# Routing of a mixture-of-experts block: one product for channels and logits, and choices marked by GpSimd

## The chip, the cores and the metric

The kernel runs on one core of one Trainium2 chip. The metric is the time of one execution on the device, in microseconds (us). The profile was taken by the hardware profiler in one further execution; its engines are PE (TensorE, with PEld for its weight loads), DVE (VectorE), ACT (ScalarE), POOL (GpSimd) and SP (SyncE, which issues DMAs).

## The reference

The input is a batch of 32 images of 128 channels and 56 x 56 pixels, so 100,352 tokens of 128 channels, all in fp32. The first layer is a depthwise convolution, a layer norm over channels, and a mixture of eight experts of which each token takes two, within a capacity. The second layer is an attention within each token and a second mixture of 64 experts. The change touches only how the first mixture chooses its experts:

```python
x = (x - mu) / jnp.sqrt(var + 1e-06) * ln_gamma + ln_beta
xf = x.reshape(T, C)
logits = xf @ Wg + bg
topv, topi = jax.lax.top_k(logits, K)          # K = 2 of E = 8
wts = jax.nn.softmax(topv, axis=-1)
priority = wts[:, 0]
order = jnp.argsort(-priority)
...
cap = int(CAP_RATIO * T / E)
pos = ...   # place of each choice in its expert, in order of priority
keep = pos < cap
```

A token has a place in an expert only if it is among the first `cap` tokens of that expert by priority.

## The kernel before, in words

The kernel has stages that follow each other. The convolution writes its channels to `conv_d` in device memory. Routing reads them back and finds each token's logits and its two experts. A selection stage then finds, by a search of 24 steps, the priority from which each expert keeps its tokens. After it come the scattering of tokens to experts, the experts, and the second layer.

Routing works on groups of seven tiles of 128 tokens, 112 groups in all. The generator `route(g)` writes the work of one group in steps that are parted by `yield`; `in_turn` starts one new group in each round and advances every group under way by one step, the oldest first. The steps before the change are:

1. load the group's channels into `ct` (L358, SyncE's queue, four buffers);
2. for each tile, multiply it with `jm` (L364), the matrix that takes off the mean over channels, into PSUM tiles `pc` of four and three tiles; ScalarE squares them and sums (`sq` L372 for four tiles, `sqs` L367 for three, which VectorE sums at L368) into `ss`; and multiply each tile again, with the eight columns of `rw` for the logits (L377), into the PSUM tile `pl`;
3. the inverse root of the variance, in `inverse`: three steps on ScalarE (L143 to L145);
4. four steps on GpSimd (L147 to L150), which leave it in `rst`;
5. VectorE multiplies `pl` by `rst` (L381) and adds the bias `cb` (L382), which gives the logits `lgs`;
6. VectorE finds the largest values (L387) and their indices (L389), tile by tile, and ScalarE copies the first two of each into `pk` (L390, L391).

In all these products the tile of `ct` is the stationary operand, which is loaded, and `jm` or `rw` is streamed. Before the groups, a few products of the weights set up `rw` and `cb` (L345 to L351, through the PSUM tile `pa`).

The selection stage takes the values and indices from `pk`. It computes the share and the priority of every token (`ex`, `den`, `share`, `prio`, L405 to L413; the negative largest logit `negl` on GpSimd, L410), and then for each expert a row of keys, `key[:, e, :]`, which holds the priority where the expert is one of the token's two and zero elsewhere (L418, L419, L422), less a constant (L423, ScalarE). The search counts over these rows (L447, L452).

Within an engine, instructions run in the order in which the scheduler of the framework put them, which weighs the steps of different groups against each other; waits between engines are semaphores that it places. PSUM tiles and SBUF tiles of a pool are buffers in turn, and a new use waits for the last reader of the old one.

Of the kernel before, what the change touches and what calls it, by code (L numbers as in the profile page):

```python
# [8 lines left out]
F32 = mybir.dt.float32  # L9
I32 = mybir.dt.int32  # L10
U32 = mybir.dt.uint32
AF = mybir.ActivationFunctionType
ALU = mybir.AluOpType
AX = mybir.AxisListType
# [3 lines left out]
P = 128  # L18
GJ = 7
# [6 lines left out]
def conv_attn_hybrid_kernel(  # L26
# [24 lines left out]
    nc = tc.nc  # L51
    N, C, H, W = x.shape
    HW = H * W
    T = N * HW
    E = Wg.shape[1]
# [19 lines left out]
    TC = T // P  # L75
# [43 lines left out]
    def over(t, n):  # L119
        return t.unsqueeze(2).to_broadcast([t.shape[0], t.shape[1], n])  # L120

    def across(t, n):
        return t.unsqueeze(1).to_broadcast([t.shape[0], n, t.shape[1]])
# [12 lines left out]
    def by_tile(t):  # L136
        return t.rearrange("c (j p) -> c j p", p=P)
# [61 lines left out]
    with tc.tile_pool(name="cv_c", bufs=1) as cc, tc.tile_pool(  # L199
        name="cv", bufs=3  # L200
# [20 lines left out]
        for c in range(C):  # L221
# [15 lines left out]
            for kw in range(KS):  # L237
                for r in range(2):
                    rows = slice(r * HP, r * HP + H)
                    for b in range(2):  # L240
# [4 lines left out]
                            start=(kw == 0),  # L245
                            stop=(kw == KS - 1),
# [17 lines left out]
    RO = C + C + E  # L264
    CHUNKS = ((0, 4), (4, GJ))
# [5 lines left out]
    rst = ch.tile([P, TC], F32, name="rst")  # L271
    lgs = ch.tile([P, TC, E], F32, name="lgs")
# [37 lines left out]
    count = ch.tile([P, P // E], F32, name="count")  # L310
# [7 lines left out]
    rw = ch.tile([C, RO], F32, name="rw")  # L318
    cb = ch.tile([P, C + E], F32, name="cb")

    pairs = ExitStack()
    pk = pairs.enter_context(tc.tile_pool(name="pairs", bufs=1)).tile([P, TC, 4], F32, name="pk")
    with tc.tile_pool(name="rt_c", bufs=1) as cc, tc.tile_pool(
        name="rt", bufs=4
    ) as rt, tc.tile_pool(name="rt_p", bufs=2, space=PSUM) as rtp:
        tc.keep_in_program_order(
            nc.scalar.preload_act_table_set("natural_log_exp_and_others")
        )
        gam = cc.tile([C, 1], F32, name="gam")
        nc.sync.dma_start(gam, ln_gamma.unsqueeze(1))  # L330
        nc.sync.dma_start(bet, ln_beta.unsqueeze(1))
        wg = cc.tile([C, E], F32, name="wg")
        nc.sync.dma_start(wg, Wg)
        bgt = cc.tile([P, E], F32, name="bgt")
        nc.sync.dma_start(bgt, bg.partition_broadcast(P))

        jm = cc.tile([C, C], F32, name="jm")
        nc.vector.tensor_scalar(jm, ident, 1.0 / C, None, ALU.subtract)
        raw = cc.tile([C, RO], F32, name="raw")
        nc.vector.tensor_copy(raw[:, :C], ident)  # L340
        nc.vector.tensor_copy(raw[:, C : C + C], turn)
        nc.vector.tensor_copy(raw[:, C + C :], wg)

        ps = rtp.tile([P, RO], F32, name="pa", bufs=1)
        nc.tensor.matmul(ps, bet.to_broadcast([C, P]), raw, start=True, stop=True)  # L345
        nc.vector.tensor_copy(cb[:, :C], ps[:, :C])
        nc.vector.tensor_tensor(cb[:, C:], ps[:, C + C :], bgt, ALU.add)
        nc.vector.tensor_scalar(raw, raw, gam, None, ALU.mult)
        ps = rtp.tile([P, RO], F32, name="pa", bufs=1)
        nc.tensor.matmul(ps, jm, raw, start=True, stop=True)  # L350
        nc.vector.tensor_copy(rw, ps)  # L351

        def route(g):
            pr, gl = divmod(g, GPP)
            cols = slice(g * GJ, (g + 1) * GJ)
            ct = rt.tile([C, GT], F32, name="ct")
            for im, px, col, n in segments(gl):
                nc.sync.dma_start(ct[:, col : col + n], conv_d[2 * pr + im, :, px : px + n])  # L358
            yield
            ss = rt.tile([P, GJ], F32, name="ss")  # L360
            for i, (j0, j1) in enumerate(CHUNKS):
                ps = rtp.tile([P, 4, C], F32, name="pc", bufs=4)
                for j in range(j0, j1):
                    nc.tensor.matmul(ps[:, j - j0, :], by_tile(ct)[:, j, :], jm, start=True, stop=True)  # L364
                if i:
                    sq = rt.tile([P, GJ - 4, C], F32, name="sqs", bufs=2)
                    nc.scalar.activation(sq, ps[:, : j1 - j0, :], AF.Square)  # L367
                    nc.vector.tensor_reduce(ss[:, j0:j1], sq, AX.X, ALU.add)  # L368
                else:
                    for j in range(j0, j1):  # L370
                        sq = rt.tile([P, C], F32, name="sq", bufs=2)
                        nc.scalar.activation(  # L372
                            sq, ps[:, j - j0, :], AF.Square, accum_out=ss[:, j : j + 1]
                        )
            pl = rtp.tile([P, GJ, E], F32, name="pl")
            for j in range(GJ):
                nc.tensor.matmul(pl[:, j, :], by_tile(ct)[:, j, :], rw[:, C + C :], start=True, stop=True)  # L377
            yield
            yield from inverse(rt, ss, 0, "rst", 3, rst[:, cols])
            lg = lgs[:, cols, :]  # L380
            nc.vector.tensor_tensor(lg, pl, over(rst[:, cols], E), ALU.mult)  # L381
            nc.vector.tensor_tensor(lg, lg, across(cb[:, C:], GJ), ALU.add)  # L382
            yield
            m8 = rt.tile([P, GJ, 8], F32, name="m8")
            i8 = rt.tile([P, GJ, 8], U32, name="i8")
            for j in range(GJ):
                nc.vector.max(m8[:, j, :], lg[:, j, :])  # L387
            for j in range(GJ):
                nc.vector.max_index(i8[:, j, :], m8[:, j, :], lg[:, j, :])  # L389
            nc.scalar.copy(pk[:, cols, 0:2], m8[:, :, 0:2])  # L390
            nc.scalar.copy(pk[:, cols, 2:4], i8[:, :, 0:2])  # L391

        in_turn(route(g) for g in range(NG))

    with tc.tile_pool(name="sel", bufs=1) as se, tc.tile_pool(
        name="sel2", bufs=2
# [1 line left out]


        HALF = 2.0**23
        ea = [pk[:, :, 2], pk[:, :, 3]]
        ex = se.tile([P, TC], F32, name="ex")
        nc.vector.tensor_tensor(ex, pk[:, :, 1], pk[:, :, 0], ALU.subtract)  # L405
        nc.scalar.activation(ex, ex, AF.Exp)
# [4 lines left out]
        prio = se.tile([P, TC], F32, name="prio")  # L411
# [3 lines left out]
        nc.vector.memset(less, -HALF)  # L415
        key = se.tile([P, E, TC], F32, name="key")
        for e in range(E):
            nc.vector.tensor_scalar(key[:, e, :], ea[0], float(e), None, ALU.is_equal)  # L418
            nc.vector.scalar_tensor_tensor(  # L419
                key[:, e, :], ea[1], float(e), key[:, e, :], ALU.is_equal, ALU.add  # L420
            )
            nc.vector.tensor_tensor(key[:, e, :], key[:, e, :], prio, ALU.mult)  # L422
            nc.scalar.activation(key[:, e, :], key[:, e, :], AF.Identity, bias=less)  # L423

        def total(cnt):
# [13 lines left out]
        for b in range(1, 25):  # L439
            step = 2.0 ** (24 - b)  # L440
            off = s2.tile([P, E - EV], F32, name="off")
# [4 lines left out]
            for e in range(EV):  # L446
                nc.vector.tensor_scalar(  # L447
                    junk[0], key[:, e, :], cand[:, e : e + 1], None, ALU.is_ge, ALU.add,
                    accum_out=cnt[:, e : e + 1],
                )  # L450
            for e in range(EV, E):
                nc.scalar.activation(  # L452
                    junk[1], key[:, e, :], AF.Sign, bias=off[:, e - EV : e - EV + 1],
                    accum_out=cnt[:, e : e + 1],
# [21 lines left out]
        for e in range(E):  # L476
            k = key[:, e, :]
            eq = se.tile([P, TC], F32, name=f"eq{e}")
            if e < 5:
# [3 lines left out]
                    accum_out=ngt[:, e : e + 1],  # L483
# [47 lines left out]
        ps = sep.tile([P, JB, E], F32, name="gram", tag="tot")  # L531
# [11 lines left out]
        ps = sep.tile([P, E, E], F32, name="sizes", tag="tot")  # L543
# [1055 lines left out]
```

## Time and profile before

| | |
|---|---|
| time, median of 3 runs | 9506.17 us (9501.17 to 9524.23) |
| time of the profiled execution | 9507.39 us |
| its span, first to last instruction | 9505.7 us |
| PE busy, share of the span | 8565.6 us, 90% |
| PEld busy | 6983.3 us, 73% |
| DVE busy | 6481.0 us, 68% |
| ACT busy | 5277.1 us, 56% |
| POOL busy | 6777.5 us, 71% |
| convolution, from the timeline | 0 to 703 us |
| routing | 703 to 1073 us |
| keys of the selection | 1073 to 1108 us |
| rest of the selection and start of the scatter | 1108 to 1330 us |

The shares of the whole span mix stages with different limits. The edited code runs only from 703 to 1108 us, so the stretch to read is that one, and in it the engine that is never idle.

### The profile page before, as it was taken

The page shows a single profiled execution, that of the slowest core. Times are in us where ns is not written, and L with a number is a line of the kernel's source. Part 1 is how long each engine was busy: PE and PEld are TensorE (multiplying, and loading weights), DVE is VectorE, ACT ScalarE, POOL GpSimd, SP SyncE. Part 2 cuts the span into 40 slices and gives each one's busy share as a digit, 9 for nine tenths or more (in the row PEclk, how much of TensorE's full clock was granted, in tenths as well). Part 3 has the DMA queues.
Part 4 walks back from the last instruction along what each step waited for, and adds up shares of the span by engine and source line. Part 5 has one row for each costly group of instructions (what it writes and reads, how often), then busy time and mean ns, then how long its engine had stood idle before and what let it go on. Part 6 is the DMA issues. An engine that isn't in the chain of part 4 may idle for free. (4 is left out here: it accounts for less than half of the span.)

```text
span 9505.7 us, 165321 instructions
## 1 busy us (share of the span) xinstructions
PE 8565.6 (90%) x62216; PEld 6983.3 (73%) x62216; DVE 6481.0 (68%) x10957; ACT 5277.1 (56%) x13401; POOL 6777.5 (71%) x4884
## 2 busy tenths in 40 slices
PE   9999558775999999998999999999999999999878
PEld 3459546554766666666889899988989988989733
DVE  1117889885222222225999999999999999999623
ACT  1116644332333333334788888888888888888600
POOL 0002137777787777777999999999999999999500
PEclk9999779998999999999999999999999999999865
DMA  9994238775444444442000000000000000000199
GB/s 205 213 205 142 70 103 226 209 210 150 77 62 71 71 69 69 70 65 39 25 31 31 31 28 26 29 31 31 31 31 25 29 30 31 31 31 31 62 317 336
DMA packets 996146, 849.92 MB, mean 89 GB/s; under 512 B 525013, under 2 KB 880664, under 8 KB 975859
## 3 DMA queue, kind: packets, MB, share of 16 engines
q1 hardware_dynamic: 470162, 494.25, 18.6%
q0 software_dynamic: 177664, 188.81, 11.5%
q10 hardware_dynamic: 347520, 156.28, 6.1%
q8 instruction: 493, 8.08, 0.4%
q14 instruction: 307, 2.51, 0.1%
HBM read 486.34 MB, written 353.64 MB: 88 GB/s over the span
## 5 line engine op out<-in xcount | busy, mean ns | idle before, releaser
L161 POOL TENSOR_TENSOR s<-s,q 128x2048 f32<-128x2048 f32 x784 | 3601.9, 4605 | 137.8 <-DVE s L161 107.5
L161 ACT ACTIVATE s<-s 128x2048 f32<-128x2048 f32 x784 | 1500.8, 1914 | 685.9 <-POOL s L161 682.2
L161 POOL DMA_INDIRECT t_d<-ys,xe x992 | 1530.5, 1543 | 409.2 <-issue 229.0
L161 DVE TENSOR_TENSOR s<-kv,c 128x2048 f32<-128x2048 f32 x784 | 1786.5, 2279 | 8.0 <-POOL c L161 8.0
L161 DVE TENSOR_TENSOR ev<-s,kv 128x2048 f32<-128x2048 f32 x784 | 1784.0, 2276 | 2.4 <-ACT s L161 2.4
L161 PE MATMUL sm<-ident,ev 128*128 128x128 f32 x12544 | 1530.6, 276 | 45.4 <-DVE ev L161 45.4
L161 PE MATMUL sm<-ident,s 128*128 128x128 f32 x12544 | 1526.1, 275 | 8.5 <-ACT s L161 8.5
L161 PEld LDWEIGHTS sm<-ident,ev 128*128 128x128 f32 x12544 | 1436.3, 144 | 92.8 <-DVE ev L161 50.6
L161 PEld LDWEIGHTS sm<-ident,s 128*128 128x128 f32 x12544 | 1405.0, 143 | 20.8 <-ACT s L161 8.7
L888 ACT ACTIVATE hT<-ph,b1t 128x512 f32<-128x512 f32 (+1 forms) x992 | 679.3, 685 | 1236.5 <-PE ph L884 1220.8
L899 DVE TENSOR_TENSOR ys<-py,b2t 128x512 f32<-128x512 f32 (+1 forms) x248 | 171.4, 691 | 1545.9 <-PE py L894 1454.2
L894 PEld LDWEIGHTS py<-w,hT 128*128 128x128 f32 x7936 | 960.6, 192 | 202.1 <-issue 91.5
L894 PE MATMUL py<-w,hT 128*128 128x128 f32 x7936 | 984.6, 278 | 0.2
L884 PE MATMUL ph<-xeT,w 128*128 128x512 f32 (+1 forms) x1984 | 921.3, 597 | 69.5 <-DVE xeT L880 69.5
L697 POOL DMA_INDIRECT xb_d<-xs,rd x784 | 766.5, 978 | 240.2 <-issue 199.2
L241 PE MATMUL cps<-xin,br 56*64 56x448 f32 x7168 | 687.5, 541 | 13.6 <-DVE br L235 11.1
L884 PEld LDWEIGHTS ph<-xeT,w 128*128 128x128 f32 x1984 | 348.3, 190 | 392.0 <-issue 293.2
L241 PEld LDWEIGHTS cps<-xin,br 56*64 56x64 f32 x7168 | 334.0, 132 | 366.4 <-issue 331.2
L161 PE MATMUL pa<-rw,ct 128*128 128x256 f32 x1568 | 393.4, 393 | 127.6 <-DVE xs L161 127.5
L287 POOL MEMSET code<- 128x64 f32 x1 | 0.2, 151 | 697.4 <-DMA conv_d<-ot 697.4
L161 PEld LDWEIGHTS pa<-rw,ct 128*128 128x128 f32 x1568 | 283.7, 194 | 261.0 <-DVE xs L161 172.0
L161 PE MATMUL kv<-wq,zT 128*128 128x256 f32 x1568 | 417.2, 389 | 52.7 <-DVE ev L161 52.3
(330 smaller groups left out, 13264.5 us busy)
## 6 DMA issues: line engine op xcount, KB each, us to landing
ct<-conv_d SPq DMA_DIRECT2D x192, 448.0 KB
xin<-in_x_dram SPq DMA_DIRECT2D x256, 196.0 KB
conv_d<-ot ACTq DMA_DIRECT2D x512, 98.0 KB
t_d<-xs ACTq DMA_DIRECT2D x112, 448.0 KB
tr<-t_d SPq DMA_DIRECT2D x112, 448.0 KB
to<-t_d SPq DMA_DIRECT2D x32, 1568.0 KB
out_dram<-oo ACTq DMA_DIRECT2D x32, 1568.0 KB
xg<-in_x_dram SPq DMA_DIRECT2D x96, 448.0 KB
```

The source lines that it names most:

```text
L161: r = getattr(self.engine, name)(*a, **k)
L241: nc.tensor.matmul(pss[r][b * HP : (b + 1) * HP], br[rows, kw, :], xi[rows, b * NB : (b + 1) * NB, kw : kw + W], start=(kw == 0), stop=(kw ...
L287: nc.gpsimd.memset(code, -1.0)
L697: s = nc.gpsimd.indirect_dma_start(out=xb_d, out_offset=bass.IndirectOffsetOnAxis(ap=idx, axis=0), in_=row, in_offset=None, bounds_check=R ...
L884: nc.tensor.matmul(ph[:, :, :rows], w1[:, f * P : (f + 1) * P], xT[:, :, :rows], start=True, stop=True,)
L888: nc.scalar.activation(hT[:, f, :, :rows], ph[:, :, :rows], AF.Gelu, bias=b1t[:, f : f + 1])
L894: nc.tensor.matmul(py[:rows, j, :], hT[:, f, j, :rows], w2[:, f, :], start=(f == 0), stop=(f == NF - 1),)
L899: nc.vector.tensor_tensor(ys[:rows], py[:rows], across(b2t, SB)[:rows], ALU.add)
```

## The change

Routing makes one product for each tile instead of two. A new matrix `jl` holds `jm` and the eight logit columns of `rw` side by side, 136 columns. The PSUM tile `pc` is now a pair of banks with three tiles in each, in three buffers; the seventh tile has a PSUM tile of its own, `po`, in two buffers, which the setup products share. ScalarE squares four tiles singly (the first three and the seventh) and the other three at once, as before in number. VectorE copies the logit columns out of PSUM into `lgs`, in two copies, directly after the sums of squares. The factor `rst` and the bias `cb` are applied later, in SBUF, by GpSimd.

`pk` now holds the two values alone. The indices go, as fp32, to a small tile `ei`, and in a new last step of `route` GpSimd forms, for each token and expert, the differences of the expert's number and the two chosen numbers (`off`), and multiplies them to `hot`, which is zero where the expert was chosen. The selection then makes each key row with one VectorE instruction (is `hot` zero, times the priority) in place of three.

```diff
-    pk = pairs.enter_context(tc.tile_pool(name="pairs", bufs=1)).tile([P, TC, 4], F32, name="pk")
+    pa_ = pairs.enter_context(tc.tile_pool(name="pairs", bufs=1))
+    pk = pa_.tile([P, TC, 2], F32, name="pk")
+    hot = pa_.tile([P, TC, E], F32, name="hot")
...
-        ps = rtp.tile([P, RO], F32, name="pa", bufs=1)
+        ps = rtp.tile([P, RO], F32, name="pa", tag="po")
...
+        CE = C + E
+        jl = cc.tile([C, CE], F32, name="jl")
+        nc.vector.tensor_copy(jl[:, :C], jm)
+        nc.vector.tensor_copy(jl[:, C:], rw[:, C + C :])
+        JH = GJ // 2
...
             ss = rt.tile([P, GJ], F32, name="ss")
-            for i, (j0, j1) in enumerate(CHUNKS):
-                ps = rtp.tile([P, 4, C], F32, name="pc", bufs=4)
-                for j in range(j0, j1):
-                    nc.tensor.matmul(ps[:, j - j0, :], by_tile(ct)[:, j, :], jm, start=True, stop=True)
-                if i:
-                    sq = rt.tile([P, GJ - 4, C], F32, name="sqs", bufs=2)
-                    nc.scalar.activation(sq, ps[:, : j1 - j0, :], AF.Square)
-                    nc.vector.tensor_reduce(ss[:, j0:j1], sq, AX.X, ALU.add)
-                else:
-                    for j in range(j0, j1):
-                        sq = rt.tile([P, C], F32, name="sq", bufs=2)
-                        nc.scalar.activation(
-                            sq, ps[:, j - j0, :], AF.Square, accum_out=ss[:, j : j + 1]
-                        )
-            pl = rtp.tile([P, GJ, E], F32, name="pl")
+            pc = rtp.tile([P, 2, 512], F32, name="pc", bufs=3)
+            po = rtp.tile([P, CE], F32, name="po")
+            at_ = pc[:, :, : JH * CE].rearrange("p i (j c) -> p i j c", c=CE)
             for j in range(GJ):
-                nc.tensor.matmul(pl[:, j, :], by_tile(ct)[:, j, :], rw[:, C + C :], start=True, stop=True)
+                nc.tensor.matmul(
+                    po if j == 2 * JH else at_[:, j // JH, j % JH, :], by_tile(ct)[:, j, :], jl,
+                    start=True, stop=True,
+                )
+            for j in (*range(JH), 2 * JH):
+                sq = rt.tile([P, C], F32, name="sq", bufs=2)
+                nc.scalar.activation(
+                    sq, po[:, :C] if j == 2 * JH else at_[:, 0, j, :C], AF.Square,
+                    accum_out=ss[:, j : j + 1],
+                )
+            sq = rt.tile([P, JH, C], F32, name="sqs", bufs=2)
+            nc.scalar.activation(sq, at_[:, 1, :, :C], AF.Square)
+            nc.vector.tensor_reduce(ss[:, JH : 2 * JH], sq, AX.X, ALU.add)
+            lg = lgs[:, cols, :]
+            nc.vector.tensor_copy(
+                lg[:, : 2 * JH].rearrange("p (i j) e -> p i j e", i=2), at_[:, :, :, C:]
+            )
+            nc.vector.tensor_copy(lg[:, 2 * JH], po[:, C:])
             yield
             yield from inverse(rt, ss, 0, "rst", 3, rst[:, cols])
-            lg = lgs[:, cols, :]
-            nc.vector.tensor_tensor(lg, pl, over(rst[:, cols], E), ALU.mult)
-            nc.vector.tensor_tensor(lg, lg, across(cb[:, C:], GJ), ALU.add)
+            nc.gpsimd.tensor_tensor(lg, lg, over(rst[:, cols], E), ALU.mult)
+            nc.gpsimd.tensor_tensor(lg, lg, across(cb[:, C:], GJ), ALU.add)
...
-            nc.scalar.copy(pk[:, cols, 0:2], m8[:, :, 0:2])
-            nc.scalar.copy(pk[:, cols, 2:4], i8[:, :, 0:2])
+            nc.scalar.copy(pk[:, cols, :], m8[:, :, 0:2])
+            ei = rt.tile([P, GJ, 2], F32, name="ei")
+            nc.scalar.copy(ei, i8[:, :, 0:2])
+            yield
+            off = rt.tile([P, 2, GJ, E], F32, name="off_")
+            nc.gpsimd.tensor_tensor(
+                off, count[:, :E].unsqueeze(1).unsqueeze(1).to_broadcast([P, 2, GJ, E]),
+                ei.rearrange("p j i -> p i j").unsqueeze(3).to_broadcast([P, 2, GJ, E]),
+                ALU.subtract,
+            )
+            nc.gpsimd.tensor_tensor(hot[:, cols, :], off[:, 0], off[:, 1], ALU.mult)
...
         for e in range(E):
-            nc.vector.tensor_scalar(key[:, e, :], ea[0], float(e), None, ALU.is_equal)
             nc.vector.scalar_tensor_tensor(
-                key[:, e, :], ea[1], float(e), key[:, e, :], ALU.is_equal, ALU.add
-            )
-            nc.vector.tensor_tensor(key[:, e, :], key[:, e, :], prio, ALU.mult)
+                key[:, e, :], hot[:, :, e], 0.0, prio, ALU.is_equal, ALU.mult
+            )
             nc.scalar.activation(key[:, e, :], key[:, e, :], AF.Identity, bias=less)
```

In the changed kernel the product is L374, the squares L380 and L385, the sum of squares L386, the copies L388 and L391, factor and bias L394 and L395, maxima L400, indices L402, `off` L408, `hot` L413 and the key product L439.

More of the change, by code (lines that the diff above doesn't have):

```diff
@@ L348, in conv_attn_hybrid_kernel @@
         nc.vector.tensor_scalar(raw, raw, gam, None, ALU.mult)
-        ps = rtp.tile([P, RO], F32, name="pa", bufs=1)
+        ps = rtp.tile([P, RO], F32, name="pa", tag="po")
         nc.tensor.matmul(ps, jm, raw, start=True, stop=True)
         nc.vector.tensor_copy(rw, ps)
+        CE = C + E
[3 more added lines that the diff above has]
+        JH = GJ // 2
+        assert 2 * JH + 1 == GJ and JH * CE <= 512
         def route(g):
@@ L402, in conv_attn_hybrid_kernel @@
         HALF = 2.0**23
-        ea = [pk[:, :, 2], pk[:, :, 3]]
         ex = se.tile([P, TC], F32, name="ex")
```

## The prediction

> **What bounds the kernel now.** I first read the windows, to see how much time the edited stages have. Columns: stretch in us, length, then busy us and instruction count of PE, PEld, DVE, ACT, POOL, then clock, DMA share, GB/s.
>
> ```profile
> 703.00:1073.00 370.00, 362.13 (x3140) 361.74 (x3140) 274.67 (x2697) 248.48 (x1568) 94.46 (x513) 0.96 0.49 141
> 1073.00:1108.00 35.00, 0.00 (x0) 0.00 (x0) 34.66 (x39) 9.25 (x13) 3.37 (x6) 0.50 0.00 0
> ...
> 760.00:800.00 40.00, 40.00 (x360) 40.00 (x360) 30.87 (x310) 28.09 (x179) 10.61 (x52) 1.00 0.50 147
> ...
> 724.00:728.00 4.00, 4.00 (x21) 4.00 (x20) 2.51 (x24) 1.34 (x10) 0.81 (x4) 0.50 0.03 13
> ```
>
> Routing is 703 to 1073, building the keys 1073 to 1108. In steady routing TensorE has no idle time; the DMA is half used. The groups of instructions from 760 to 1060 say who waits (last column: idle time before the group, and what ended it):
>
> ```profile
> L364 PE MATMUL pc<-jm,ct 128*128 128x128 f32 x1344 | 173.5, 281 | 0.0
> L377 PE MATMUL pl<-rw,ct 128*128 128x8 f32 x1345 | 156.4, 250 | 0.0
> ...
> L368 DVE TENSOR_REDUCE ss<-sqs 128x3 f32<-128x384 f32 x96 | 53.1, 553 | 61.4 <-ACT sqs L367 61.4
> L367 ACT ACTIVATE sqs<-pc 128x384 f32<-128x384 f32 x96 | 47.0, 490 | 68.3 <-PE pc L364 68.3
> ...
> L147 POOL TENSOR_TENSOR rst<-rst 128x7 f32<-128x7 f32 x96 | 19.6, 204 | 197.8 <-ACT rst L145 197.8
> ```
>
> ScalarE waits for TensorE, VectorE for ScalarE: TensorE leads. The timeline of one group of seven tiles (start, us, engine, line) gives the period and the lags:
>
> ```profile
> 900.09 1.64 PEld L377 LDWEIGHTS pl<-rw,ct 128*128 128x128 f32 x14
> ...
> 900.47 0.30 ACT L143 ACTIVATE rst<-ss,eps 128x7 f32<-128x7 f32 x1
> 900.54 0.58 DVE L387 MAX8 m<-lgs 128x8 f32<-128x8 f32 x7
> ...
> 901.26 0.22 ACT L145 ACTIVATE rst<-rst 128x7 f32<-128x7 f32 x1
> ...
> 901.55 0.20 POOL L147 TENSOR_TENSOR rst<-rst 128x7 f32<-128x7 f32 x1 [2.06 <-ACT rst L145]
> ...
> 901.65 1.64 PEld L364 LDWEIGHTS pc<-jm,ct 128*128 128x128 f32 x14
> ...
> 901.91 0.16 DVE L389 FIND_INDEX8 i<-m,lgs 128x8 uint32<-128x8 f32 x1
> ...
> 902.42 0.20 POOL L150 TENSOR_TENSOR rst<-rst 128x7 f32<-128x7 f32 x1
> ...
> 903.22 1.64 PEld L377 LDWEIGHTS pl<-rw,ct 128*128 128x128 f32 x14
> ```
>
> The period is 903.22 - 900.09 = 3.13 us. Half of it (1.57) goes to logits products of only 8 columns: each product is 14 load-and-multiply records per group, 112 ns each, and each loads the same `ct` tile again. Per group (40 us / 3.13 = 12.8 groups) VectorE is busy 30.9 / 12.8 = 2.42 us, ScalarE 2.20, GpSimd 0.83.
>
> [...] 192 ns for L364 and L377 alike, whatever the columns multiplied. [...] Here it is 0.50 from 1073 to 1108, with TensorE idle, and also at 724. [...] No such copy of these sizes is in the trace; the near rows are 206 (L381, 56 elements) and 155 (L347, 8).
>
> **The change, part by part.**
>
> *TensorE.* 14 of 28 records per group go; the others get 136 columns. The 128x256 product (L161, pa) has a median of 379 ns against 275 for 128x128: 0.81 ns a column, so 8 columns cost 6.5 ns. 14 x 118 = **1.66 us** a group. At half clock (window 724: 21 records in 4 us, 0.195 each) it would be 14 x 0.208 = 2.91.
>
> *VectorE.* L381 and L382 (0.206 + 0.217) go, two copies come: by the near rows 0.21 + 0.155[...]. 2.42 - 0.42 + 0.36 = **2.36 us**[...].
>
> *ScalarE.* The same number of squares, roots and copies: **2.20 us**.
>
> *GpSimd.* To L147 to L150 come factor, bias (56 elements each), `off` (112) and `hot` (56). The forms it runs later in the kernel are 128x16 at 226 ns, 128x128 at 403, 128x256 at 621, with broadcast operands among them; between them 56 elements are 0.29 us and 112 are 0.38, as estimates. One that reads its predecessor starts 0.08 after it (901.75 to 901.84); an independent one some 0.03 early. L147 to L150 hold 1.15, then 0.37, 0.26, 0.46 and 0.26: **2.50 us**. Bounds: 2.2 if a short one stays at L147's 0.20, 3.3 if the two-way broadcast of `off` and the eight-element rows double them.
>
> *A loop of waits.* The built program's order on VectorE is: reduce group N, copy its pc, maxima and indices of N-1, with the po copy of N+1 before the last index, reduce N+1. Maxima now wait for GpSimd, and behind them are queued the po copy, which frees a PSUM buffer that TensorE needs, and the next reduce, for which ScalarE's root waits. So from reduce N to reduce N+2: reduce 0.55, to the root 0.10, L143 to L145 1.01 (900.47 to 901.48), to GpSimd 0.07, L147 to L150 1.07, factor and bias 0.74, to VectorE 0.04, maxima and indices 1.53 (900.54 to 902.07), po copy 0.15: 5.26 us for two groups, **2.63 each**. This is longer than any engine's own work, GpSimd's 2.50 close below. I take 2.65. What is late next is this chain, and no longer TensorE.
>
> *Loads and buffers.* The `ct` loads stay 128, in SP's same order; no load moves past another. At 2.65 us a group they need 147 x 3.13 / 2.65 = 174 GB/s; the convolution's DMAs move 208. They cost nothing under that cover; if it went, they would hold a group to 3.13 x 0.50 = 1.57, still below. Three pc pairs and two po put TensorE a group ahead, so the PSUM waits cost nothing.
>
> *Start.* Products must now wait for `jl`, which needs the pa-to-rw chain: 711.82 to 714.80 before, so 3.0 and 0.2 for its copy. With `ct` there at 707.2, products start at 710.4, at half clock (7 products 2.9), squares follow (1.5): first reduce 714.8. Six groups at half clock add 6 x 0.26 = 1.5. The last reduce is 111 periods (294.2) later, the last index 5.1 after that: 714.8 + 294.2 + 1.5 + 5.1 = 1015.6 against 1073.05 now: **-57.4 us**.
>
> *Keys.* L418 and L422 (0.88 and 0.98) go eight times, L419 (1.54) stays, reading `hot` at a stride of 32 bytes instead of 16; no row reads so. I keep 1.54; the two-operand strided L405 bounds it at 2.1, 1.03 (a contiguous L514) below. From the last index now: last L422 ends at +34.0. After: `ex` also waits for GpSimd, whose last `hot` stands behind negl (1.57): +1.75. Then `ex` 1.6 (between 0.98 contiguous and 2.10; its stride falls to 8 bytes), ScalarE's exponential with its waits 1.13, which L418 covered before, den, reciprocal and prio 6.8, eight products 12.3: +23.6. **-10.4 us**, -6 to -14.
>
> **Sum.** -57.4 - 10.4 = -67.8 against the profiled execution's 9507.39 (span 9505.7); that one is 1.2 above the median, so 9506.17 - 67.8 = 9438. Later stages follow unchanged. A tenth of a us per group is 11.1 us.
>
> **Rivals.**
>
> *TensorE clocked down.* With 1.66 of 2.65 us busy it might lose its clock; for it, 0.50 in the window at 724; against it, [...]the later stage from 1330 to 2300 holds 0.97 at some 79% busy. At half clock 2.91: 9438 + 29 = 9467. Dearer GpSimd operations (+0.1 each: 2.9) end at the same place.
>
> *VectorE's own work binds*, if GpSimd's short operations stay near 0.20 and the loop shrinks: 2.38, 9438 - 30 = 9408.
>
> *Slower: GpSimd takes TensorE's place.* Break-even is 2.65 + 67.8 / 111 = 3.26 us a group. It decides from there: the four new operations would have to take 2.11 instead of 1.35. With 0.5 each for the three of 56 elements and 0.9 for `off`, plus lags, 1.15 + 2.5 = 3.65: 9438 + 111 = 9549. For it, GpSimd's rate at 2048 elements is half VectorE's, and no row has `off`'s pattern; against it, 256 elements with a broadcast take 0.62.
>
> *The merging gives nothing* (a 136-column product costing two): 3.13, only the keys gain, less the later start: about 9494. Against it, the 128x256 product at 379.
>
> **How the numbers follow.** Period 2.5 to 2.8: 0.62, 9438. VectorE's floor: 0.10. Half clock or dearer GpSimd, up to 2.99: 0.18. Periods from 3.0 to 3.5: 0.06. Above: 0.04. A measurement of this kernel tells about 0.3%, 28.5 us, from no change, so faster ends at 9478, where the period is 3.0: faster 0.90, same 0.06, slower 0.04. The range 9408 to 9478 runs from VectorE's floor to a period of 3.0, and takes in the keys' bounds.
>
> **What would show it.** Right: L374 x1568 records with a mean near 285 ns; groups 2.6 to 2.7 us apart; maxima waiting for GpSimd; TensorE some 60% busy; POOL some 2.1 us busy a group; the last index near 1016; key building 24 us. Wrong: `off` above 0.6 us or GpSimd without idle time, TensorE still without idle time, clock at 0.5 after 740, or a key product above 2 us.

## The result, and the profile after

| | before | after |
|---|---|---|
| median | 9505.73 us (14 runs, 9491.51 to 9524.23) | 9427.24 us (14 runs, 9417.63 to 9492.93) |
| ratio, 95% interval | | 0.9921 (0.9912 to 0.9930) |
| span of the profiled execution | 9505.7 us | 9415.9 us |
| first channel load of routing issued | 703.1 | 697.4 |
| first and last sum of squares start (112 groups) | 711.1, 1068.4 | 713.3, 996.7 |
| end of the last index | 1073.05 | 1002.2 |
| VectorE's first count of the search starts | 1107.2 | 1024.0 |

The change takes 78.5 us off the median; 67.8 were forecast, 9438 us. The two spans differ by more, 89.8, because in the execution profiled after, the convolution, which is not edited, ended 5.7 us earlier, and because the stages after the first count, not edited either, took 6.6 us less. What the edited code owns is therefore measured from the first channel load to the first count of the search: 404.1 us before (1107.2 - 703.1), 326.6 after (1024.0 - 697.4), 77.5 less. In the profiled executions of the kernels e5 to e8 below, the granted clock of TensorE from 1330 to 2300 us was 0.80, against 0.96 in that of after, and the kernel before, measured beside them, took 9917.84 us, so that these four are compared with that time alone.

First the windows of after, with the columns as in the prediction: routing, the keys, the 40 us shown of before, and a longer stretch of steady routing.

```profile
697.00:1002.00 305.00, 240.17 (x1572) 198.85 (x1572) 246.16 (x2697) 237.67 (x1568) 230.79 (x959) 0.97 0.58 171
1002.00:1024.00 22.00, 0.00 (x0) 0.00 (x0) 20.60 (x29) 8.52 (x11) 2.42 (x8) 0.50 0.00 0
760.00:800.00 40.00, 33.50 (x221) 27.72 (x222) 33.93 (x375) 32.96 (x220) 32.14 (x126) 1.00 0.61 182
760.00:980.00 220.00, 183.87 (x1209) 151.51 (x1210) 186.94 (x2069) 181.82 (x1210) 176.69 (x692) 1.00 0.61 182
```

TensorE was busy all of the 40 us before and is now idle for 6.5 of them, at a granted clock of 1.00. The period is (996.7 - 713.3) / 111 = 2.553 us a group. (The same sum for before gives 3.219, but there the first six gaps are 3.6 to 6.7 us; its steady groups are 3.127 apart.) No engine is busy for more than 85% of the long stretch (VectorE, 186.94 of 220), and GpSimd's busy time is only 80%: by the busy shares nothing bounds this stage. The waits of the same stretch show what does (engine, line, the line waited for: us in total, times, longest):

```profile
DVE m L400 <- POOL lgs L395: 33.1, 87, 0.6
PEld po L374 <- DVE lgs L391: 31.5, 87, 0.6
ACT rst L143 <- POOL lgs L394: 28.6, 63, 0.7
...
ACT rst L143 <- DVE ss L386: 8.9, 23, 0.4
```

All engines wait for each other: VectorE's maxima for GpSimd's bias, TensorE for VectorE's copy, ScalarE's root for VectorE's sum. (The list puts most of the root's waits down to the factor L394, because that operation ends at about the same time. But in 108 of the 112 groups the root starts 0.09 to 0.10 us after the end of the sum, and in 38 of these the factor is still running: the sum is what it waits for. The lines at 885.24 and 885.51 below show such a group.) The groups of instructions (busy us, mean ns of one, idle before) give the prices:

```profile
L374 PE MATMUL pc<-jl,ct 128*128 128x136 f32 x1035 | 140.7, 286 | 22.3 <-issue 22.0 <-ACT sq L380 0.3
...
L400 DVE MAX8 m<-lgs 128x8 f32<-128x8 f32 x604 | 49.8, 154 | 33.1 <-POOL lgs L395 33.1
L386 DVE TENSOR_REDUCE ss<-sqs 128x3 f32<-128x384 f32 x87 | 46.4, 533 | 0.0
...
L395 POOL TENSOR_TENSOR lgs<-lgs,cb 128x56 f32<-128x56 f32 x87 | 26.2, 302 | 6.8
...
L394 POOL TENSOR_TENSOR lgs<-lgs,rst 128x56 f32<-128x56 f32 x87 | 24.5, 282 | 6.9 <-POOL rst L150 0.2
...
L147 POOL TENSOR_TENSOR rst<-rst 128x7 f32<-128x7 f32 x86 | 17.9, 209 | 1.4 <-ACT rst L145 0.3
```

The product of 136 columns takes 286 ns, one of 128 took 281 before. The timeline lets the loop be walked by hand (start, us, engine, line; the idle time before it and what ended it in brackets):

```profile
882.37 0.54 DVE L386 TENSOR_REDUCE ss<-sqs 128x3 f32<-128x384 f32 x1
...
883.00 0.30 ACT L143 ACTIVATE rst<-ss,eps 128x7 f32<-128x7 f32 x1 [0.47 <-POOL lgs L394]
...
883.75 0.30 POOL L413 TENSOR_TENSOR hot<-off__9543 128x56 f32<-128x56 f32 x1
883.80 0.20 ACT L145 ACTIVATE rst<-rst 128x7 f32<-128x7 f32 x1
...
884.08 0.21 POOL L147 TENSOR_TENSOR rst<-rst 128x7 f32<-128x7 f32 x1
...
884.88 0.53 DVE L386 TENSOR_REDUCE ss<-sqs 128x3 f32<-128x384 f32 x1
...
885.24 0.28 POOL L394 TENSOR_TENSOR lgs<-lgs,rst 128x56 f32<-128x56 f32 x1
...
885.51 0.30 ACT L143 ACTIVATE rst<-ss,eps 128x7 f32<-128x7 f32 x1 [0.40 <-DVE ss L386]
...
885.60 0.30 POOL L395 TENSOR_TENSOR lgs<-lgs,cb 128x56 f32<-128x56 f32 x1
...
885.94 0.37 DVE L400 MAX8 m<-lgs 128x8 f32<-128x8 f32 x4 [0.41 <-POOL lgs L395]
```

From the sum at 882.37 to the root at 883.00 are 0.63 us, to the root's end at 884.00 another 1.00, to GpSimd 0.08, through its six operations to 885.90 another 1.82, to the maxima 0.04. From maxima to the next sum it is 1.51 (taken one group earlier: 883.37, not shown, to 884.88). Together 5.08 us, and the loop spans two groups: 2.54 each. The same lines show a second candidate. GpSimd's last mark L413 ends at 884.05 and L147 starts at 884.08: in this order GpSimd has no idle time but the lags between its operations, and its own work, some 2.51 us a group (2.54 from the start of L147 to the end of L413, less the 0.04 us by which an operation that needs nothing from its predecessor can start before that one ends), is nearly as long as the loop's share. L147 starts 0.08 us after the end of the root in nearly every group, which speaks for the loop; but the two are so close that an experiment has to decide.

### The profile page after: what moved, and what is told of

It reads as the page before. It is cut to its first block, busy times and chain, and to the rows that moved or that the text cites. A ratio compares the mean times of both kernels' runs of the same rounds, so it can differ in the third digit from the quotient of the medians.

```text
span 9415.9 us, 162622 instructions
## 1 busy us (share of the span) xinstructions
PE 8433.8 (90%) x60648; PEld 6763.7 (72%) x60648; DVE 6437.0 (68%) x10943; ACT 5265.5 (56%) x13401; POOL 6911.7 (73%) x5332
## 5 line engine op out<-in xcount | busy, mean ns | idle before, releaser
L161 POOL TENSOR_TENSOR s<-s,q 128x2048 f32<-128x2048 f32 x784 | 3601.9, 4605 | 136.1 <-DVE s L161 105.5
L241 PE MATMUL cps<-xin,br 56*64 56x448 f32 x7168 | 684.4, 540 | 11.1 <-DVE br L235 10.7
L241 PEld LDWEIGHTS cps<-xin,br 56*64 56x64 f32 x7168 | 283.5, 132 | 411.2 <-issue 410.0
```

The lines of the kernel that those rows point to most:

```text
L161: r = getattr(self.engine, name)(*a, **k)
L241: nc.tensor.matmul(pss[r][b * HP : (b + 1) * HP], br[rows, kw, :], xi[rows, b * NB : (b + 1) * NB, kw : kw + W], start=(kw == 0), stop=(kw ...
```

## The experiments

Each kernel is compared with the time of before that was measured beside it: 9509.04 us for e1 to e4, 9917.84 for e5 to e8, 9506.74 for e9 and e10. Routing keeps its periods across these sets (2.175 in e2, 2.177 in e6, which has the same order). In the table, "stage" is from the first channel load to VectorE's first count of the search (before 404.1), taken from one profiled execution of each; "period" is between sums of squares in the same way as above.

| kernel | median, us | against before | ratio (95%) | stage against before | period |
|---|---|---|---|---|---|
| after | 9427.24 | -78.5 | 0.9921 (0.9912 to 0.9930) | -77.5 | 2.553 |
| e1 no marks | 9440.94 | -68.1 | 0.9926 (0.9910 to 0.9943) | -66.6 | 2.543 |
| e2 VectorE in order | 9382.06 | -127.0 | 0.9868 (0.9852 to 0.9885) | -116.1 | 2.175 |
| e3 both | 9397.18 | -111.9 | 0.9885 (0.9868 to 0.9901) | -106.6 | 2.173 |
| e4 factor on VectorE | 9431.28 | -77.8 | 0.9916 (0.9899 to 0.9932) | -69.4 | 2.616 |
| e5 two products | 9907.15 | -10.7 | 0.9991 (0.9982 to 1.0000) | -14.0 | 3.136 |
| e6 e2, early bet | 9795.79 | -122.1 | 0.9881 (0.9865 to 0.9898) | -122.2 | 2.177 |
| e7 threshold, in order | 9783.55 | -134.3 | 0.9862 (0.9846 to 0.9879) | -138.0 | 1.994 |
| e8 e7, early bet | 9783.16 | -134.7 | 0.9861 (0.9845 to 0.9878) | -142.7 | 2.006 |

### e5: two products again

```diff
-            for j in range(GJ):
-                nc.tensor.matmul(
-                    po if j == 2 * JH else at_[:, j // JH, j % JH, :], by_tile(ct)[:, j, :], jl,
-                    start=True, stop=True,
-                )
+            for cs in (slice(0, C), slice(C, CE)):
+                for j in range(GJ):
+                    to = po if j == 2 * JH else at_[:, j // JH, j % JH, :]
+                    nc.tensor.matmul(to[:, cs], by_tile(ct)[:, j, :], jl[:, cs], start=True, stop=True)
```

> The changed kernel, but each tile is multiplied twice again: by the 128 columns of jm and by the 8 logit columns, into the same PSUM places. Everything behind the product (copies, factor and bias on GpSimd, marks, keys) stays as changed. Theory P (the number of products is what the change took off, and TensorE is the bound again if it comes back): 28 load-and-multiply records of 112 ns a group, 3.13 us, TensorE without idle time; against the kernel before only the keys (-12) and the later start (+4) remain: about 9497. Rival M (the merging is worth little, since the loop of waits and the shorter stages behind it set the pace): 2.55 us a group, about 9430. Between them: each tenth of a us per group is 11 us.

Steady routing, windows and groups:

```profile
760.00:940.00 180.00, 180.00 (x1614) 180.00 (x1614) 130.48 (x1387) 121.06 (x810) 118.39 (x461) 1.00 0.51 148
```

```profile
L376 PE MATMUL pc<-jl,ct 128*128 128x8 f32 (+1 forms) x1382 | 172.2, 266 | 0.0
```

TensorE is without idle time again, 3.136 us a group (3.127 in steady routing, as in before), and the gain in routing is gone. What is left, -14.0 in the stage and -10.7 in the time, is mostly the keys: from the last index to the end of the last key product it is 21.9 us in e5, as in after, against 34.0 in before, -12.1. The rest nearly cancels: the first sum comes 6.2 us later after the first load (14.2 against 8.0), the gaps between the sums then take 9.3 us less, since the first groups are not so far apart as in before, and the last index comes 1.4 us later after the last sum. Theory P holds. The number of products, far more than their columns, was TensorE's price: in e5's timeline the fourteen records of 128 columns take 1.64 us (they start at 900.91, the next at 902.55) and the fourteen of 8 columns the other 1.50, while a load of the tile takes 192 ns by its median for either (L364 and L377 of before). And all of the change's gain in routing comes from it; nothing else that it moves saves time while TensorE is the bound.

### e1: GpSimd without the marks

The two operations `off` and `hot` go; values and indices are kept in `pk` and the keys are made as before (two comparisons and a product for each expert).

```diff
-            off = rt.tile([P, 2, GJ, E], F32, name="off_")
-            nc.gpsimd.tensor_tensor(off, ..., ALU.subtract)
-            nc.gpsimd.tensor_tensor(hot[:, cols, :], off[:, 0], off[:, 1], ALU.mult)
...
+            nc.vector.tensor_scalar(key[:, e, :], ea[0], float(e), None, ALU.is_equal)
             nc.vector.scalar_tensor_tensor(
-                key[:, e, :], hot[:, :, e], 0.0, prio, ALU.is_equal, ALU.mult
+                key[:, e, :], ea[1], float(e), key[:, e, :], ALU.is_equal, ALU.add
             )
+            nc.vector.tensor_tensor(key[:, e, :], key[:, e, :], prio, ALU.mult)
```

> The changed kernel with the marking taken back: indices go into pk as before, off and hot are gone from GpSimd, the keys are built by the three old VectorE instructions. GpSimd's own work falls from some 2.5 us a group to some 1.8; VectorE's order (maxima of group N-1 between the sums of N and N+1) stays. Theory L (the loop of waits sets the period, 5.08 us for two groups in the changed kernel): the period stays at 2.54 and only the keys get dearer, by 12 us: some 9439 against 9427. Theory G (GpSimd's own work sets it): the period falls to VectorE's own work, 2.43, a gain of 12 us that eats the keys' loss: some 9427.

The waits of its steady routing, and three sums of its timeline:

```profile
POOL rst L147 <- ACT rst L145: 51.3, 71, 1.2
ACT rst L143 <- DVE ss L385: 26.8, 44, 0.9
DVE m L399 <- POOL lgs L394: 26.7, 45, 0.8
```

```profile
879.80 0.53 DVE L385 TENSOR_REDUCE ss<-sqs 128x3 f32<-128x384 f32 x1
...
882.05 0.54 DVE L385 TENSOR_REDUCE ss<-sqs 128x3 f32<-128x384 f32 x1
...
884.88 0.53 DVE L385 TENSOR_REDUCE ss<-sqs 128x3 f32<-128x384 f32 x1
```

GpSimd now idles for 51.3 of 180 us before L147, and the period stays: 2.543. The sums come here 2.25 and 2.83 us apart in turn, and two groups take 5.08 us, the loop's length to the hundredth. That is the loop alone, with GpSimd's own work taken away (1.81 us from L147 to the end of the bias). The median is 13.7 us above after's, 10.4 when each is taken against the time of before beside it, about what the old keys cost (-12.1 in reverse).

### e2 and e3: the order of VectorE

`vo` is an engine handle that holds VectorE's instructions of routing in the order in which they are written. No instruction is added or removed.

```diff
+        vo = InOrder(nc.vector)
...
-            nc.vector.tensor_reduce(ss[:, JH : 2 * JH], sq, AX.X, ALU.add)
+            vo.tensor_reduce(ss[:, JH : 2 * JH], sq, AX.X, ALU.add)
```

and so for both copies, maxima and indices. e3 is e1 with this edit.

> The changed kernel, only that VectorE's instructions in the route keep the order of the text: after the sum of squares and both copies of group N come maxima and indices of N-3, not N-1. The loop of waits then spans four groups, some 1.3 us each, so it no longer binds; the scheduler puts off and hot between L147 and L150, which hides start lags and takes GpSimd to some 2.2 us. Theory L and theory V (VectorE's own 2.43 us comes next): period 2.43 to 2.45, 10 to 13 us less than the changed kernel, some 9415. Theory G: period between 2.2 and 2.5 as GpSimd's work falls; then GpSimd would show no idle time.

> Both edits together: marking taken back and VectorE in the order of the text. Theories L and V: period 2.43, VectorE without idle time, and the old keys cost 12 us: some 9427. If the period falls clearly below 2.4, VectorE's own work was overestimated; if it stays at 2.54, neither GpSimd nor the loop was the bound.

Windows of steady routing of e1, e2 and e3, in this order:

```profile
760.00:940.00 180.00, 145.84 (x998) 123.85 (x996) 152.13 (x1696) 149.43 (x997) 99.82 (x427) 1.00 0.63 183
```

```profile
760.00:940.00 180.00, 153.91 (x1160) 139.80 (x1161) 175.44 (x1989) 172.97 (x1159) 156.73 (x657) 1.00 0.75 213
```

```profile
760.00:940.00 180.00, 153.93 (x1160) 139.81 (x1161) 175.39 (x1989) 173.00 (x1159) 116.08 (x497) 1.00 0.75 213
```

Lines of e2's timeline, the copies and maxima of VectorE and the factor of every second group on GpSimd:

```profile
879.94 0.28 POOL L396 TENSOR_TENSOR lgs<-lgs,rst 128x56 f32<-128x56 f32 x1
...
881.75 0.20 DVE L161 COPY lgs<-pc 128x48 f32<-128x48 f32 x1
881.86 0.16 DVE L161 COPY lgs<-po 128x8 f32<-128x8 f32 x1
881.93 0.57 DVE L161 MAX8 m<-lgs 128x8 f32<-128x8 f32 x7
...
884.33 0.28 POOL L396 TENSOR_TENSOR lgs<-lgs,rst 128x56 f32<-128x56 f32 x1
```

e3 against e1 is the clean pair, since GpSimd has slack in both: the order takes the period from 2.543 to 2.173. (The scheduler also moved ScalarE's copies into `pk` among the steps of the root; that was not held fixed.) In the trace of e2 the maxima that follow the copies of group N are those of N-3, whose bias GpSimd finished long before; the wait of 33.1 us at the maxima is gone, VectorE is busy for 97% and ScalarE for 96%, and the loop is cut. With the marks (e2 against after) it is the same, 2.553 to 2.175. There GpSimd's order moved along: it now puts `off` and `hot` between the operations of another group. Of the sixteen operations of two groups seven come directly behind the one whose result they read, where in after it was twelve, and the eight of a group take (884.33 - 879.94) / 2 = 2.19 us between starts of the factor, in place of 2.51. At 2.51, GpSimd's own work would be longer than e2's period. I had expected 2.43 of VectorE and about 9415 us; its own work is smaller than I had put it.

### e4: factor and bias on VectorE

```diff
-            nc.gpsimd.tensor_tensor(lg, lg, over(rst[:, cols], E), ALU.mult)
-            nc.gpsimd.tensor_tensor(lg, lg, across(cb[:, C:], GJ), ALU.add)
+            nc.vector.tensor_tensor(lg, lg, over(rst[:, cols], E), ALU.mult)
+            nc.vector.tensor_tensor(lg, lg, across(cb[:, C:], GJ), ALU.add)
```

> The changed kernel with factor and bias applied by VectorE in SBUF instead of GpSimd. Theory V: VectorE has 2.43 + 2 x 0.22 = 2.87 us a group and becomes the bound: period 2.85 to 2.9, some 9427 + 111 x 0.33 = 9463. Theory L: the loop loses the two GpSimd operations (0.73) and gains 0.5 on VectorE, so it would fall a little, to some 2.45, and the time with it; that would show VectorE with idle time.

```profile
760.00:940.00 180.00, 136.13 (x957) 117.59 (x958) 162.01 (x1781) 148.71 (x960) 99.89 (x410) 1.00 0.61 176
```

The period is 2.616, between what the theories gave: VectorE is busy for 90% and still waits for GpSimd, 18.0 of 180 us, now for `rst` at the factor's line. The time, -77.8 against before, cannot be told from after's; the stage is 8.1 us longer (-69.4 against -77.5). The edit is not clean, though: with it the scheduler also put the maxima of group N-2, no longer of N-1, behind the sum of N. What e4 shows is that as built the two places of the factor differ by no more than that; what the place alone is worth in one fixed order stays open.

### e6: the start

```diff
+    bet = const.tile([C, 1], F32, name="bet")
+    nc.sync.dma_start(bet, ln_beta.unsqueeze(1))
...
-    bet = ch.tile([C, 1], F32, name="bet")
...
-        nc.sync.dma_start(bet, ln_beta.unsqueeze(1))
```

The first pair stands at the start of the kernel; VectorE is in order as in e2.

> The changed kernel with VectorE's instructions of routing in the order of the text (as in e2_vector_order), and the load of bet, a column of 128 values that the setup products of the weights need, issued at the start of the kernel instead of behind the first four loads of channels. Theory S (the setup products wait for that load, and the first group for them): the first product and the first sum of squares come 3 to 4 us earlier after the first channel load, the period stays at 2.17; 9378 against the 9382 of e2. Rival R (the setup chain is held by something else, the channels or TensorE at half clock): first sum of squares 15 to 16 us after the first channel load as in the changed kernel, 9382.

First the start of routing in after: SyncE's issues, the setup products L347 and L352, `jl`, the first product and the first sum of squares.

```profile
697.42 1.78 SPq L367 DMA_DIRECT2D ct<-conv_d  x4
...
699.38 0.56 SPq L333 DMA_DIRECT2D bet<-in_L_conv_ln_beta_dram  x1
...
704.67 1.22 PE L347 MATMUL pa<-raw,bet 128*128 128x264 f32 x2 [9.21 <-DMA ct<-conv_d]
...
708.37 0.17 DVE L358 COPY jl<-rw 128x8 f32<-128x8 f32 x1
708.60 3.09 PE L374 MATMUL pc<-jl,ct 128*128 128x136 f32 x12 [0.73 <-DVE jl L358]
...
713.27 0.55 DVE L386 TENSOR_REDUCE ss<-sqs 128x3 f32<-128x384 f32 x1 [0.21 <-ACT sqs L385]
```

Then e6:

```profile
696.77 0.68 PE L347 MATMUL pa<-raw,bet 128*128 128x264 f32 x2 [0.87 <-DVE ot L257]
...
697.88 18.03 SPq L369 DMA_DIRECT2D ct<-conv_d  x11
...
702.80 3.09 PE L376 MATMUL pc<-jl,ct 128*128 128x136 f32 x12 [3.65 <-DVE jl L358]
```

In after the idle time before L347 is put down to a channel load, though this product does not read `ct`: `bet`, which it reads, was issued behind those loads on the same queue. In e6 the setup product runs 1.1 us before the first channel load is issued. The first sum of squares comes 9.6 us after that load (707.5 - 697.9), against 16.1 in e2 and 15.9 in after. Theory S holds, and the gain of the stage is 6.1 us over e2 (-122.2 against -116.1), more than expected. The times do not show it (-122.1 against -127.0, each against another time of before): so little cannot be told from them.

### e7 and e8: marks by a threshold

```diff
-            i8 = rt.tile([P, GJ, 8], U32, name="i8")
...
-                nc.vector.max_index(i8[:, j, :], m8[:, j, :], lg[:, j, :])
...
-            nc.scalar.copy(ei, i8[:, :, 0:2])
...
-            nc.gpsimd.tensor_tensor(off, ..., ALU.subtract)
-            nc.gpsimd.tensor_tensor(hot[:, cols, :], off[:, 0], off[:, 1], ALU.mult)
+            nc.gpsimd.tensor_tensor(
+                hot[:, cols, :], lg, m8[:, :, 1:2].to_broadcast([P, GJ, E]), ALU.subtract
+            )
...
-                key[:, e, :], hot[:, :, e], 0.0, prio, ALU.is_equal, ALU.mult
+                key[:, e, :], hot[:, :, e], 0.0, prio, ALU.is_ge, ALU.mult
```

VectorE is in order; e8 has the early `bet` as well.

> VectorE in the order of the text, and no indices: instead of finding the indices of the two largest logits (seven VectorE instructions a group), turning them into fp32 (ScalarE) and forming off and hot from them (two GpSimd instructions), GpSimd subtracts the second largest logit from the eight logits, and the key product asks whether the difference is at least zero. Where the second and third logit of a token are exactly equal, three experts are marked instead of two. Theory A (after e2 VectorE and ScalarE are both at their own work, 2.12 and 2.09 us; VectorE loses about 1.0 us and ScalarE its copy of the indices, 0.15 to 0.2): ScalarE or GpSimd binds at 1.95 to 2.05 us a group, 9382 - 15 to 25 = 9357 to 9367. Rival W (a loop of waits is left: maxima wait for GpSimd, GpSimd for ScalarE, ScalarE for VectorE's sums): the period stays near 2.17 with no engine above 90%, 9382.

> e6 and e7 together: VectorE in the order of the text, no indices (three experts marked where the second and third logit are exactly equal), bet loaded at the start of the kernel. If the two effects are of different stages they add up: e7's time less 3 to 4 us, about 9355 to 9364, and below both kernels; if e6 shows nothing, e7's time.

```profile
760.00:940.00 180.00, 155.88 (x1219) 146.70 (x1218) 113.75 (x893) 176.36 (x1155) 143.78 (x626) 0.99 0.75 219
```

```profile
880.16 0.21 ACT L145 ACTIVATE rst<-rst 128x7 f32<-128x7 f32 x1
...
881.38 0.29 POOL L404 TENSOR_TENSOR hot<-lgs,m 128x56 f32<-128x56 f32 x1
881.63 0.20 POOL L147 TENSOR_TENSOR rst<-rst 128x7 f32<-128x7 f32 x1
```

In e7 VectorE falls to 63%, ScalarE is at 98%, and the period is 1.994: theory A, which named ScalarE or GpSimd. Which of the two it is, the trace does not say. GpSimd is busy for 80%, but it never waits: in the lines above L147 starts before `hot` has ended and 1.26 us after the end of the root that it reads (1.0 or 1.3 us in most groups), and the only gaps on GpSimd are the 0.08 us between operations that read one another. It takes 21.9 us off the stage against e2 (-138.0 and -116.1). e8's stage is 4.7 us shorter than e7's, of the 3 to 4 expected, but its time is the same within the runs' spread. Both are faster than either kernel of the case.

### e9 and e10: what `ex` pays

`ex`, the difference of the two logits, took 2.10 us before, 0.98 after, and 1.64 in e7, which has after's operands. In e7's timeline it lies beside GpSimd's `negl`. Both kernels move `negl` to ScalarE, e9 in the kernel before, e10 in e7:

```diff
-        nc.gpsimd.tensor_scalar(negl, pk[:, :, 0], -1.0, 0.0, ALU.mult, ALU.add)
+        nc.scalar.activation(negl, pk[:, :, 0], AF.Copy, scale=-1.0)
```

> The kernel before, but negl, which GpSimd computes from pk at the time when VectorE computes ex from it, is computed by ScalarE. Theory C (in the kernel before, ex waits for negl: both read pk with GpSimd and VectorE at once, and ex took 2.10 us of which 0.68 lay beside negl): ex takes 1.4 us here. Rival D (the 2.10 us are the price of two operands at a stride of 16 bytes): ex stays at 2.10. The whole time moves by a us at most, within noise.

> The kernel of e7 (VectorE in the order of the text, no indices, three experts marked where second and third logit are exactly equal), with negl computed by ScalarE instead of GpSimd. In e7 ex took 1.64 us beside negl, in the changed kernel 0.98 after it, with the same operands at a stride of 8 bytes. Theory C (overlap with GpSimd's negl is what ex pays): ex 0.98 us. Rival D (something else in this order lengthens it): 1.64. The whole time moves by a us at most, within noise.

Instructions of the tile `ex` in before, e9, e7 and e10 (minimum, median and maximum ns, then first and last start):

```profile
L405 DVE TENSOR_TENSOR ex<-pk x1: 2104/2104/2104, 1073.3 to 1073.3; 128x784 f32<-128x784 f32 x1
```

```profile
L405 DVE TENSOR_TENSOR ex<-pk x1: 1550/1550/1550, 1065.3 to 1065.3; 128x784 f32<-128x784 f32 x1
```

```profile
L419 DVE TENSOR_TENSOR ex<-pk x1: 1644/1644/1644, 945.0 to 945.0; 128x784 f32<-128x784 f32 x1
```

```profile
L419 DVE TENSOR_TENSOR ex<-pk x1: 975/975/975, 951.2 to 951.2; 128x784 f32<-128x784 f32 x1
```

With `negl` elsewhere `ex` takes 1550 ns at a stride of 16 bytes and 975 at 8; beside it, 0.55 and 0.67 us more. In e10 `ex` lies beside `negl` on ScalarE (951.11 to 952.06) and pays nothing, so what counts is that GpSimd does it, and not that another engine reads the same tile. Theory C holds, with 1.55 in place of the 1.4 that I expected. In the traces of before and e7 `negl` had started first, and it ended 0.68 us after the start of `ex` in before (1072.43 + 1.57 against 1073.32) and 0.81 in e7, where `ex` took 0.55 and 0.67 us more; `negl` itself took 883 ns in e7, as in after (882), where it ran before `ex`: in e7 only `ex` paid. How GpSimd holds VectorE up was not shown. The time of the whole kernel tells nothing here (one execution each: 9500.27 us for e9, 9376.57 for e10, 9506.74 for before).

## Why the prediction was right

**Sign, mechanism and size.** The median came 10.8 us below the forecast of 9438 and lies within its range. The bound named was the loop of waits over two groups at 2.63 us each; it is there, at 2.54, and e1 and e3 show that it is the bound. That the sum came so close is in part luck: the terms below are off in both directions. Product price (285 ns named, 286 measured), full clock, and loads that cost nothing (182 GB/s in steady routing, and 213 in e2, whose waits name none of them) are as forecast; e5 gives back the price of two products. What I called close below, GpSimd's own 2.50, is some 2.51. TensorE waits 31.5 us for the copy of `po`, which I had put at a group ahead, but the sums behind its products have no idle time before them (L386), so these waits cost nothing, as forecast.

**The signs.** Of those named for right, the mean of a product, the maxima waiting for GpSimd and GpSimd's 2.05 us a group came as said; groups were 2.55 apart, not 2.6 to 2.7, the keys took 21.9 us, not 24, and the last index came 304.8 us after the first load, not 312.5 (1015.6 - 703.1). TensorE was busy for 84%, not 60%: its fourteen records stand for 2.13 us a group (two for 0.50 and twelve for 1.63 in the timeline), not 1.66; the work comes in two stretches, and most of the difference, by my estimate, is that each ends with a record at its full 0.28 us (L374's median is 279 ns) where 0.118 a record had been put. And one sign named for wrong did come: GpSimd has no idle time but its lags. e1 shows that it was not the bound all the same.

**The terms that were mis-sized**, with the sum from the first channel load, where -67.8 had been split into -57.4 and -10.4:

- *Period*, 111 times 2.65 and 1.5 for the clock at the start, 295.7: measured 283.4, **-12.3**. I had worked out 2.63 and rounded up to 2.65; the loop is 5.08 in place of 5.26. The difference sits in the stretch from maxima to the next sum, which I had at 1.53 and 0.15 one behind the other; with the copy between the indices it is 1.51. And TensorE was at half clock for less than two groups, not for six (0.50 from 708 to 712 us, 0.87 from 712 to 716, 1.00 from 716 to 720): twelve records took 3.09 us, the next twelve of the same tile 2.10, the next 1.55.
- *Start*, 11.7 us from first load to first sum: measured 15.85, **+4.1**. The step that was off is "products must now wait for `jl`, which needs the pa-to-rw chain: 3.0 and 0.2", with the chain starting when `ct` is there. The chain starts with `bet`, issued 1.96 us after the first of four channel loads on the same queue, and it ran at half clock (0.50 from 704 to 708 us; 1.22 us for the setup product, against 0.68 in e6, where it ran at 696.77 and the first 700 us are at 1.00). In before `bet` stood in the same place (issued at 705.05), but the setup product at 711.82 was queued behind the first products, which hid it. e6 takes 6.5 us off by moving that load.
- *After the last sum*, 5.1 us: measured 5.5, **+0.4**.
- *Keys*, 23.6 us from the last index: measured 21.9, **-1.7**. `ex` at 0.98, not 1.6, gives -0.6; the wait for the last `hot`, 1.17 in place of 1.75, another -0.6; and the eight products, one behind the other in 11.92 us in place of 12.3, -0.4. The step that was off is the bound of `ex`: 2.10 was taken as the price of a stride, and e9 shows that 0.55 of it was `negl`.

These sum to -9.5, so that -67.8 becomes -77.3, as the stage shows (-77.5).

**VectorE's own work**, 2.36 us, was the worst number of the text, though it did not enter the forecast: e2 runs at 2.175 with all of it. The copies are 198 and 147 ns by their medians (206 and 155 by the near rows of before), so the durations were fair. But an independent instruction starts some 0.1 us before its predecessor ends (the copy of `pc` at 882.82, the sum before it ending at 882.91): in e2's lines the two copies take 0.18 us of the engine's time, from 881.75 to the maxima at 881.93, and not 0.36. The rest of the difference stays open; that the removed factor and bias, of which each waits for the one before, had taken more room than their durations is likely, but was not isolated. It matters since the rival "VectorE's own work binds" was put at 9408 as a floor, 98 us below before: e2 lies 127 below it.

**The rivals.** TensorE clocked down: 1.00 in steady routing, gone. The merging gives nothing: e5 is that kernel, and sits at 3.136, 10.7 us below before. (The 9494 forecast for it stands without a sum: -10.4 for the keys and 3.7 for the start give about 9499, the terms of the start with 3.13 for the period about 9492.) GpSimd takes TensorE's place: `off` takes 383 to 388 ns, 0.38 forecast, and factor, bias and `hot` 282, 302 and 304 against 0.29; far from the 2.11 us for the four at which it would have decided. (GpSimd's half of VectorE's rate at 2048 elements, named for this rival, is 4605 ns against 2276 to 2279 for a two-input operation in before.)

## What to carry to other kernels

When a change relieves the bounding engine, walk the built order for a loop of waits through several engines before taking the next busiest engine as the bound: here no engine was over 85% busy, taking work off an engine that the loop passes through gave routing nothing (e1), and putting one engine's instructions in another order gave some 45 us (e2). Of two operations that had ended before the root started, the list of waits named the later one here (the factor at 882.95 us, not the sum at 882.91): compare starts and ends over many groups before believing it. A duration taken over from a row of the profile can carry what ran beside that row (0.55 us of the 2.10 of `ex`): look at the other engines' timeline at that moment before reading it as a price. And when a setup result moves ahead of the first product, follow its chain back to the DMA queue, where it may stand behind loads that did not matter before.

## What the runs showed of the hardware

- VectorE's subtraction of two columns of `pk` (784 elements): 974 to 977 ns at a stride of 8 bytes, 1550 at 16 (e9); beside GpSimd's `negl`, which reads the same tile, 1644 at 8 (e7) and 2076 to 2104 at 16 (before, e1, e3). Beside ScalarE's reading of the same tile it stays at 975 (e10).
- GpSimd's `negl` on 784 elements takes 882 ns at a stride of 8 bytes (after) and 1.57 us at 16 (before, always partly beside `ex`; at 8 bytes it takes 883 beside `ex` too, in e7); the key product, which reads `hot` at a stride of 32 bytes, takes 1565, like L419 at 16 (1549).
- On GpSimd the order matters at this size: eight operations of 7 to 112 elements take some 2.51 us where six of them stand directly behind the one whose result they read (after), and 2.19 with two groups interleaved (e2). Such an operation starts 0.08 us after its predecessor ends, another one 0.04 before.
